# A recurrent gate's state part as seven block products: TensorE work, setup on GpSimd, and a new start order in a graph network kernel

## Chip, cores and metric

The kernel runs on one core of one Trainium2 chip. The metric is the device time of that core in microseconds (us), the median of several runs. All data are 32-bit floats.

## The reference

There are 128 graphs of 128 nodes with 256 features. Three graph attention layers come first, then a gated graph network of three steps. Each of the four layers works on a normalised copy and adds its result to `x`.

```python
h = jnp.maximum(_layernorm(x, axis=-1), 0.0)
x = x + _L0_gnn_ref(h, adj, ...)          # attention, three times with own weights
...
def _gru_cell(inp, h, w_ih, w_hh, b_ih, b_hh):
    gi = inp @ w_ih.T + b_ih
    gh = h @ w_hh.T + b_hh
    i_r, i_z, i_n = jnp.split(gi, 3, axis=-1)
    h_r, h_z, h_n = jnp.split(gh, 3, axis=-1)
    r = jax.nn.sigmoid(i_r + h_r)
    z = jax.nn.sigmoid(i_z + h_z)
    n = jnp.tanh(i_n + r * h_n)
    return (1.0 - z) * n + z * h
...
for i in range(L):                        # L = 3
    m = jnp.einsum('bnd,de->bne', h, weight[i])
    aggr = jnp.einsum('bst,bsd->btd', A, m)
    h = _gru_cell(aggr, h, w_ih, w_hh, b_ih, b_hh)
```

The term `h_n`, the state's part of the candidate gate, is what the change is about. It is a product of the state (256 features by nodes) with a 256 x 256 matrix.

## The kernel before

**Groups.** Batches are handled in 33 groups: one of two batches, 31 of four, one of two. A group of four has 4 x 128 = 512 columns, so a step of the recurrent network on it is a full step; the two small groups have 256 columns and take half steps. There are 93 full and 6 half steps. Groups are counted from 0, so the third group is g = 2.

**Attention** (`attention`, three layers a group): statistics of x (bn_stats on VectorE, `ve` and `rs` on GpSimd, `nm` on VectorE), normalised rows `xn` on ScalarE, scores `scr`, a spread of one score row over the partitions through DRAM (`de`, `er`), softmax on `em`, a transpose through DRAM (`d_at`, `at`), the products `ahp` and `hp` on TensorE, and the addition to x. The first two groups do their transposes on TensorE instead of through DRAM. After the third layer the rows are normalised once more to `hn`. For g = 0 they are turned on TensorE, for the others through DRAM (`tr_h`, `d_h`, `h<-d_h`), and `flat` (L857) copies the result to the state `h` in rows of features.

**A step** (`step` inside `gru`): `aggregate` makes `agp` and its copy `ag`; `gates` (L940) makes the two gates r and z; `hidden_n` (L980) makes `h_n` in two banks `nn`; `candidate` (L1006) adds the products of `ag` to r times h_n in the banks `ni`; then the mixing gives the new state. Between steps the state goes through DRAM (`tr_hn`, `d_hn`, `hn`).

The gates use a scheme of seven block products. Weights are cut into 2 x 2 blocks of 128 x 128, the columns of h into two halves of H = 256. Instead of eight block products there are seven, of sums and differences of blocks. The combined weights are made once in the setup (`combinations`, blocks 0 to 6 of `whh_rz` and `wc_rz`). The differences of the data (`t13`, `t24`) are made for each step. The partial sums are formed in the PSUM banks a, e and b: a copy of one bank to another (L1058), a copy to s7 (L1063), two sums on VectorE (L1066, L1072) and accumulating products. `h_n` is made directly: for each of two output halves two products of 512 columns (K = 256 in two parts).

**PSUM.** Eight banks: two "gat", three "gru" (a, e, nn), two "seed" (b, ni), one "tr". A seed bank has been marked once, so that products add to what another engine wrote into it.

**Order.** Every operation is recorded with an engine, a cost and a rank, and a planner (`Plan.issue`) lays out the instructions of each engine in advance: of the operations that could start within 0.1 us of the first, the one of lowest rank is taken. No operation is taken whose rank is more than `AHEAD` above the lowest one still open. Buffers are rings: a value takes a slot when its last user is done. Ranks come from `start(g, i) = 3 g + 2 i` for the steps and `3 g - lead(g) + 2 l` for the attention, with `LEADS` for the first groups and `LEAD` for the rest; `quick = rank - URGENT` serves the short operations between products. Each engine then runs its own list in order.

Of the kernel before, what the change touches and what calls it, by code (L numbers as in the profile page):

```python
# [39 lines left out]
class Plan:  # L40
# [6 lines left out]
    WINDOW = 0.1  # L47
    AHEAD = 6.0

# [136 lines left out]
def kernel(  # L186
# [53 lines left out]
    def const_val(name, shape):  # L240
        return plan.val(const, name, 1, lambda: const.tile([P, *shape], FT, name=name))
# [21 lines left out]
    def dve(cols):  # L263
        return 0.145 + cols / 960
# [85 lines left out]
    def blocks_of(name):  # L350

        rz = const_val(f"{name}_rz", [7, 2 * P])
        n = const_val(f"{name}_n", [KD, D])
        raw = val(su, "raw", [KD, 2 * D], f"{name}_raw")
        return rz, n, raw
# [13 lines left out]

    def combinations(blocks):  # L370

        rz, n, raw = blocks

        def low(k):
            return raw.t[:, k, :].rearrange("p (g c o) -> p g c o", g=2, c=KD)[:, :, 0, :]

        def of(i):
            return rz.t[:, i, :].rearrange("p (g o) -> p g o", g=2)

        def both(i, a, b, op, reads):  # L380
            return add("DVE", dve(D), SETUP, lambda: nc.vector.tensor_tensor(
                of(i), a(), b(), op=op), reads=reads, writes=[(rz, i)])

        return [
            both(4, lambda: low(0), lambda: low(1), OP.add, [raw]),
            both(6, lambda: of(0), lambda: low(0), OP.subtract, [(rz, 0), raw]),
            both(5, lambda: of(4), lambda: of(0), OP.subtract, [(rz, 4), (rz, 0)]),
            both(2, lambda: of(1), lambda: of(5), OP.subtract, [(rz, 1), (rz, 5)]),
            add("DVE", dve(D), SETUP, lambda: nc.vector.tensor_scalar(
                of(3), low(1), -1.0, None, op0=OP.mult), reads=[raw], writes=[(rz, 3)]),  # L390
        ]
# [32 lines left out]
    def hidden():  # L424
        blocks = blocks_of("whh")
        ld, _ = loaded(w_hh, "whh")

        def part(k):
            ps = bank("gru", f"whh_{k}")
            turned_rows(ps, ld, k, 0, 4, blocks)  # L430
            kept(ps, k, blocks, "whh")
            pn = bank("gru", f"whhn_{k}")
            turned_rows(pn, ld, k, 4, 2, blocks)
            add("ACT", act(D), SETUP, lambda: nc.scalar.mul(
                blocks[1].t[:, k, :], pn.t[:, :D], 0.25), reads=[pn], writes=[(blocks[1], k)])

        for k in range(KD):
            part(k)
        return blocks

    WHH = hidden()
    combinations(WHH)
    wih = val(su, "wih", [KD, O3], "wih", bufs=1)
    transposed(w_ih, wih, "wih")

    def combined(i):
        gt = val(su, "gt", [KD, D], f"gt_{i}")
        transposed(gweight[i], gt, f"gt{i}")
        blocks = blocks_of(f"wc_{i}")

        def product(ps, m, o0, n):
            def one(k):
                add("PE", pe(n), SETUP, lambda: nc.tensor.matmul(
                    ps.t[:, :n], gt.t[:, k, m * P : (m + 1) * P], wih.t[:, k, o0 : o0 + n],
                    start=(k == 0), stop=(k == KD - 1),
                ), reads=[gt, wih], writes=[ps], takes=blocks)

# [12 lines left out]
        return blocks, [part(m) for m in range(KD)] + combinations(blocks)  # L470

    WC, last_setup = [], []
    for i in range(STEPS):
# [104 lines left out]
    def attention(g, l, xt, cap):  # L578

        name, n = f"{g}_{l}", SIZES[g]  # L580
        rank = 3.0 * g - lead(g) + 2.0 * l
        xn = val(gw, "xn", [G, D], f"xn_{name}", bufs=XN, cut=n)
# [169 lines left out]
    def gat(g):  # L752
        b0, n = FIRST[g], SIZES[g]
        rank = 3.0 * g - lead(g)
        xt = val(grp, "x", [G, D], f"x_{g}", bufs=5, cut=n)
        adj_t = val(grp, "adj", [G, N], f"adj_{g}", dtype=I32, cut=n)
# [10 lines left out]
        for l in range(3):  # L767
            attention(g, l, xt, cap)
        rank = 3.0 * g - lead(g) + 5.5
        hn = val(gw, "xn", [G, D], f"hn_{g}_0", bufs=XN, cut=n)  # L770
# [43 lines left out]
    def gru(g, xt, am, hn0, h0):  # L814
# [48 lines left out]
        def step(i, h):  # L863
# [15 lines left out]
            s7, c22 = (val(None, v, [T], f"{v}_{name}", bufs=1) for v in ("s7", "c22"))  # L879
            nn = [bank("gru", f"nn_{name}_{c}") for c in range(KD)]  # L880
            ni = [bank("seed", f"ni_{name}_{c}") for c in range(KD)]
# [20 lines left out]
            def sums(v, tag, at):  # L902
# [29 lines left out]
                }  # L932

            def gates(ps, blk, what, at, early, starts, takes=()):

# [40 lines left out]

            def hidden_n(c):
                for k in range(KD):
                    def fn(k=k):
                        nc.tensor.matmul(  # L980
                            nn[c].t[:, :TG], WHH[1].t[:, k, c * P : (c + 1) * P], h.t[:, k, :TG],
                            start=(k == 0), stop=(k == KD - 1))
                    op = add("PE", pe(TG), rank + NNR + 0.04 * c, fn, reads=[WHH[1], (h, k)],
                        writes=[nn[c]], after=gone, takes=[*takes, wn[c]])
                    if k == 0:
                        begun.append(op)
                cn = 2 * KD + c
                add("ACT", act(TG) + 0.05, quick, lambda: nc.scalar.activation(
                    wn[c].t[:, :TG], nn[c].t[:, :TG], AF.Identity, bias=bh.t[:, cn : cn + 1]
                ), reads=[nn[c], bh], writes=[wn[c]])  # L990

# [61 lines left out]
            for k in range(KD):  # L1053
# [5 lines left out]
                reads=[a], writes=[b], after=seeds)  # L1059
            for c in range(KD):  # L1060
                hidden_n(c)
            gates(e, 6, "t3", rank + 0.15, rank + 0.12, True)
# [28 lines left out]
        def end(h):  # L1091
            rank = start(g, STEPS - 1) + 1.5
            far = g < NG - FAR
# [28 lines left out]

    URGENT = 2.0
    XN = 4
    begun, seeded = [], []
    RB, ZB, NB, HB, H0 = 2, 2, 2, 2, 2
    NNR = 0.3
    LEAD = 8.50
    LEADS = [9.00, 9.50, 8.00, 8.00, 7.75, 7.75]

    def lead(g):

        return LEADS[g] if g < len(LEADS) else LEAD

    def start(g, i):

        return 3.0 * g + 2.0 * i

# [44 lines left out]
```

## Time and profile before

| what | value |
|---|---|
| median of 3 runs | 2620.41 us (2620.08 to 2621.71) |
| profiled execution | 2615.51 us |
| its span, first to last instruction | 2613.7 us |
| TensorE busy | 2569.9 us |
| VectorE, ScalarE, GpSimd busy | 2048.0, 1732.4, 216.2 us |
| products of h_n (L980) | 792 records, 379.3 us |
| mean granted TensorE clock | 0.992 |

One product of 32-bit floats leaves two records of TensorE. Records overlap, since products are pipelined, so the distance from start to start says more than the mean duration. In the lists of instructions, "idle before" is the time in which the engine stood still just ahead of the group, with the instruction that ended it. In the windows view PEclk is the granted clock as a share of the full one.

### The profile page before, as it was taken

To read this page: it belongs to the slowest core of one execution; us is meant where nothing else is said; L and a number is where in the kernel's file an instruction comes from. 1 tells how busy PE (TensorE), PEld (TensorE's weight loads), DVE (VectorE), ACT (ScalarE), POOL (GpSimd) and SP (SyncE) were. 2 spreads that over 40 slices of the span, in tenths; PEclk is the share of its full clock that TensorE was granted. 3 is DMA by queue.
4 is the path that set the end of the run, shared out by engine and by line. 5 is a ranking of instruction groups with operands and counts; after the bars stand their busy time and mean duration, and the time that the engine had idled before them with its cause. 6 is when DMAs were issued, how large, how long until landed. Compare 5 with 4: busy or idle time off the path is not lost.

```text
span 2613.7 us, 37277 instructions
## 1 busy us (share of the span) xinstructions
PE 2569.9 (98%) x11955; PEld 1994.0 (76%) x11955; DVE 2048.0 (78%) x4777; ACT 1732.4 (66%) x4112; POOL 216.2 (8%) x303
## 2 busy tenths in 40 slices
PE   8898999999999999999999999999999999999998
PEld 5776777777777777777777777777777777777777
DVE  6776878888878888878888878888878888877654
ACT  6766666766666766666766666776666766665544
POOL 1100000000010100010100010100010100000000
PEclk8998999999999999999999999999999999999999
DMA  3122334333433433333433433433333433333320
GB/s 104 49 57 65 105 105 114 98 92 93 111 100 105 109 90 94 111 100 104 109 92 92 111 101 102 109 97 89 110 101 105 106 97 91 108 91 90 74 61 13
DMA packets 503114, 245.63 MB, mean 94 GB/s; under 512 B 280579, under 2 KB 472067, under 8 KB 502918
## 3 DMA queue, kind: packets, MB, share of 16 engines
q1 hardware_dynamic: 502918, 243.25, 35.1%
q8 instruction: 95, 1.56, 0.3%
q14 instruction: 101, 0.83, 0.1%
HBM read 139.28 MB, written 103.87 MB: 93 GB/s over the span
## 4 chain that ended last, share of the span: by engine, by line
PE 92%; ACT 1%; DMA 0%; DVE 0%; SPq 0%; issue 0%; DVEq 0%; ACTq 0%
PE b L940 19%; PE a L940 12%; PE e L940 12%; PE ni L1006 12%; PE nn L980 12%; PE hp L728 12%; PE agp L966 6%; PE ahp L709 6%; DMA at<-d_at 0%; DMA er<-de 0%; SPq L549 0%; PE hnp L838 0%; ACT em L652 0%; ACT xn L588 0%; ACT em L665 0%
## 5 line engine op out<-in xcount | busy, mean ns | idle before, releaser
L980 PE MATMUL nn<-h,whh_n 128*128 128x512 f32 (+1 forms) x792 | 379.3, 581 | 0.1
L1006 PE MATMUL ni<-ag,wc_n 128*128 128x512 f32 (+1 forms) x792 | 361.8, 580 | 1.5 <-DVE ni L1000 1.5
L728 PE MATMUL hp<-w,ah 128*128 128x256 f32 x1536 | 361.6, 382 | 0.2 <-ACT ah L716 0.2
L728 PEld LDWEIGHTS hp<-w,ah 128*128 128x128 f32 x1536 | 282.4, 190 | 43.9 <-ACT ah L716 6.9
L966 PEld LDWEIGHTS agp<-am,hn 128*128 128x128 f32 x1536 | 228.6, 192 | 98.5 <-issue 80.8
L596 DVE SCALAR_TENSOR_TENSOR scr<-xn,va 128x256 f32<-128x256 f32 x732 | 271.2, 418 | 34.9 <-ACT xn L588 34.5
L966 PE MATMUL agp<-am,hn 128*128 128x128 f32 x1536 | 237.0, 276 | 6.9 <-ACT ag L974 3.6
L940 PE MATMUL a<-h,whh_rz 128*128 128x256 f32 (+1 forms) x792 | 209.9, 376 | 9.0 <-DVE h L857 8.8
L1006 PEld LDWEIGHTS ni<-ag,wc_n 128*128 128x128 f32 x792 | 140.6, 191 | 97.3 <-issue 87.3
L511 POOL TENSOR_SCALAR ve<-st 128x4 f32<-128x4 f32 (+1 forms) x132 | 39.8, 301 | 2079.9 <-DVE st L505 1475.5
L742 ACT ACTIVATE t<-hp 128x512 f32<-128x512 f32 x192 | 104.6, 595 | 156.0 <-PE hp L728 153.0
L588 ACT ACTIVATE xn<-x,nm,rs 128x256 f32<-128x256 f32 x366 | 200.6, 591 | 4.5 <-DVE nm L517 4.0
L1011 ACT ACTIVATE wn<-ni,bi 128x512 f32<-128x512 f32 (+1 forms) x198 | 133.5, 674 | 104.1 <-PE ni L1006 100.7
L940 PE MATMUL a<-ag,wc_rz 128*128 128x256 f32 (+1 forms) x792 | 200.6, 375 | 0.0
L709 PEld LDWEIGHTS ahp<-at,xn 128*128 128x128 f32 x1536 | 184.8, 192 | 15.1 <-issue 6.2
L980 PEld LDWEIGHTS nn<-h,whh_n 128*128 128x128 f32 x792 | 149.8, 191 | 59.9 <-issue 44.0
L709 PE MATMUL ahp<-at,xn 128*128 128x128 f32 x1536 | 188.4, 275 | 4.5 <-DMA at<-d_at 2.7
L744 DVE SCALAR_TENSOR_TENSOR x<-hp,x 128x512 f32<-128x512 f32 x192 | 124.1, 686 | 86.5 <-ACT t L742 86.3
L1000 DVE SCALAR_TENSOR_TENSOR ni<-r,wn 128x512 f32<-128x512 f32 (+1 forms) x198 | 135.1, 683 | 58.1 <-ACT r L994 44.9
L635 ACT ACTIVATE em<-er,e 128x128 f32<-128x128 f32 x366 | 172.3, 521 | 5.1 <-DMA er<-de 5.1
L505 DVE BATCH_NORM_STATS2 st<-x 128x6 f32<-128x512 f32 x256 | 172.1, 689 | 2.7 <-DMA x<-in_x_dram 2.6
L652 ACT ACTIVATE em<-em,nmx 128x128 f32<-128x128 f32 x384 | 149.4, 392 | 34.1 <-DVE nmx L648 33.9
(138 smaller groups left out, 5016.0 us busy)
## 6 DMA issues: line engine op xcount, KB each, us to landing
d_hn<-tr_hn SPq DMA_DIRECT2D x116, 256.0 KB, 2.4
hn<-d_hn SPq DMA_DIRECT2D x464, 64.0 KB, 2.5
er<-de SPq DMA_DIRECT2D x90, 256.0 KB, 4.4
d_at<-tr_at SPq DMA_DIRECT2D x90, 256.0 KB, 2.0
at<-d_at SPq DMA_DIRECT2D x360, 64.0 KB, 2.0
x<-in_x_dram SPq DMA_DIRECT2D x31, 512.0 KB, 5.6
d_h<-tr_h SPq DMA_DIRECT2D x31, 512.0 KB, 2.8
h<-d_h SPq DMA_DIRECT2D x124, 128.0 KB, 2.8
```

The lines of the kernel that those rows point to most:

```text
L505: add("DVE", dve(T), rank, lambda: nc.vector.bn_stats(st.t[:, b, :].rearrange("p b s -> p (b s)"), xt.t[:, b, :].rearrange("p b d -> p d b ...
L588: add("ACT", 0.45, rank, lambda: nc.scalar.activation(xn.t[:, b, :], xt.t[:, b, :], AF.Relu, bias=nm.t[:, b : b + 1], scale=rs.t[:, b : b ...
L596: add("DVE", dve(D), rank, lambda: nc.vector.scalar_tensor_tensor(scr.t, xn.t[:, b, :], 1.0 if far else rs.t[:, b : b + 1], VA[l].t[:, s, ...
L635: add("ACT", 0.55 if far else 0.42, rank, lambda: nc.scalar.activation(em.t[:, b, :], e2_row(b), AF.Prelu, bias=e.t[:, 0, b : b + 1], alph ...
L652: add("ACT", 0.42, rank, lambda: nc.scalar.activation(em.t[:, b, :], em.t[:, b, :], AF.Exp, bias=nmx.t[:, b : b + 1], accum_out=sm.t[:, b ...
L709: add("PE", pe(P), rank, lambda: nc.tensor.matmul(summed(ps, b), xn.t[:, b, k * P : (k + 1) * P], turned_weights(b), start=True, stop=True ...
L728: add("PE", pe(D), rank, lambda: nc.tensor.matmul(hp.t[:, b * D : (b + 1) * D], ah.t[:, k, c * P : (c + 1) * P], W[l].t[:, k, :], start=(k ...
L940: nc.tensor.matmul(ps.t[:, gate * D : gate * D + H], w[0].t[:, blk, gate * P : (gate + 1) * P], rhs(), start=go, stop=w is not WHH, skip_g ...
L966: nc.tensor.matmul(ps.t[:, b * P : (b + 1) * P], s, am.t[:, b, :], start=True, stop=True)
L980: nc.tensor.matmul(nn[c].t[:, :TG], WHH[1].t[:, k, c * P : (c + 1) * P], h.t[:, k, :TG], start=(k == 0), stop=(k == KD - 1))
L1000: op = add("DVE", dve(TG), quick, lambda: nc.vector.scalar_tensor_tensor(ni[c].t[:, :TG], r[c].t[:, :TG], 1.0, wn[c].t[:, :TG], op0=OP.add ...
L1006: add("PE", pe(TG), rank + 0.45 + 0.05 * c, lambda k=k: nc.tensor.matmul(ni[c].t[:, :TG], WC[i][1].t[:, k, c * P : (c + 1) * P], ag.t[:, k ...
```

## The change

- `h_n` is made by the same scheme of seven products of 256 columns, in one "gru" bank (`ae`) and one "seed" bank (`bb`), with two copies on ScalarE, two sums on VectorE and three activations of 256 columns in place of two of 512.
- `combinations` also makes the blocks of the candidate gate from w_hh, and runs on GpSimd instead of VectorE.
- The order: `AHEAD` 6 to 3.5, `URGENT` 2 to 1, `LEADS` for the first ten groups (the third from 8.0 to 10.5), layers 2.25 apart instead of 2, new starts for the first four groups, six buffers of x instead of five, four of wn instead of two.

```diff
-    AHEAD = 6.0
+    AHEAD = 3.5
...
-        n = const_val(f"{name}_n", [KD, D])
+        n = const_val(f"{name}_n", [7, P] if name == "whh" else [KD, D])
...
-    def combinations(blocks):
+    def combinations(to, raw, gates):
...
-            return add("DVE", dve(D), SETUP, lambda: nc.vector.tensor_tensor(
-                of(i), a(), b(), op=op), reads=reads, writes=[(rz, i)])
+            return add("POOL", pool(gates * P), SETUP, lambda: nc.gpsimd.tensor_tensor(
+                of(i), a(), b(), op=op), reads=reads, writes=[(to, i)])
...
+        raw_n = val(su, "raw_n", [KD, D], "whh_raw_n", bufs=1)
...
             add("ACT", act(D), SETUP, lambda: nc.scalar.mul(
-                blocks[1].t[:, k, :], pn.t[:, :D], 0.25), reads=[pn], writes=[(blocks[1], k)])
+                raw_n.t[:, k, :], pn.t[:, :D], 0.25), reads=[pn], writes=[(raw_n, k)])
+            add("ACT", act(P), SETUP, lambda: nc.scalar.mul(
+                n.t[:, k, :], pn.t[:, P : 2 * P], 0.25), reads=[pn], writes=[(n, k)])
...
-        return blocks
-
-    WHH = hidden()
-    combinations(WHH)
+        return blocks, combinations(rz, raw, 2) + combinations(n, raw_n, 1)
+
+    WHH, last_setup = hidden()
...
-        rank = 3.0 * g - lead(g) + 2.0 * l
+        rank = 3.0 * g - lead(g) + SPAN * l
...
-        xt = val(grp, "x", [G, D], f"x_{g}", bufs=5, cut=n)
+        xt = val(grp, "x", [G, D], f"x_{g}", bufs=6, cut=n)
...
-            nn = [bank("gru", f"nn_{name}_{c}") for c in range(KD)]
+            s7n = val(None, "s7n", [D], f"s7n_{name}", bufs=1)
+            ae, bb = bank("gru", f"nn_{name}"), bank("seed", f"nnb_{name}")
...
-            def hidden_n(c):
-                for k in range(KD):
-                    def fn(k=k):
-                        nc.tensor.matmul(
-                            nn[c].t[:, :TG], WHH[1].t[:, k, c * P : (c + 1) * P], h.t[:, k, :TG],
-                            start=(k == 0), stop=(k == KD - 1))
...
+            def hidden_n():
...
+                at = rank + NNR
+                one(ae, 0, 0, "11", at, True, takes)
+                one(ae, D, 6, "t3", at, False)
+                add("ACT", act(H), quick, lambda: nc.scalar.copy(bb.t[:, :H], ae.t[:, :H]),
+                    reads=[ae], writes=[bb], after=seeds)
+                add("ACT", act(H), quick, lambda: nc.scalar.copy(s7n.t[:, :H], ae.t[:, D : D + H]),
+                    reads=[ae], writes=[s7n])
+                one(bb, 0, 5, "t2", at + 0.01, False)
+                one(ae, 0, 1, "21", at + 0.02, False)
+                keep(1, 0, ae, 0)
+                add("DVE", dve(H), quick, lambda: nc.vector.tensor_add(
+                    ae.t[:, D : D + H], bb.t[:, :H], s7n.t[:, :H]), reads=[bb, s7n], writes=[ae])
+                one(bb, 0, 4, "t1", at + 0.03, False)
+                add("DVE", dve(H), quick, lambda: nc.vector.scalar_tensor_tensor(
+                    wn[0].t[:, H : 2 * H], bb.t[:, :H], bias(0), s7n.t[:, :H], op0=OP.add, op1=OP.add,
+                ), reads=[bb, s7n, bh], writes=[(wn[0], 1)])
+                one(ae, D, 3, "t4", at + 0.04, False)
+                keep(0, 0, ae, D)
+                one(bb, 0, 2, "22", at + 0.05, False)
+                keep(1, 1, bb, 0)
...
-    URGENT = 2.0
+    URGENT = 1.0
+    BASES = [0.00, 3.00, 6.00, 9.00]
+    GAPS = [2.00, 2.00, 2.25, 2.00]
+    SPAN = 2.25
+    HEAD = 5.5
+    TAIL = 1.5
...
-    RB, ZB, NB, HB, H0 = 2, 2, 2, 2, 2
-    NNR = 0.3
-    LEAD = 8.50
-    LEADS = [9.00, 9.50, 8.00, 8.00, 7.75, 7.75]
+    RB, ZB, NB, HB, H0 = 2, 2, 4, 2, 2
+    NNR = 0.25
+    LEAD = 8.5
+    LEADS = [7.50, 9.00, 10.50, 7.00, 7.75, 7.25, 8.50, 8.50, 8.50, 8.50]
...
-        return 3.0 * g + 2.0 * i
+        return BASES[g] + GAPS[g] * i if g < len(BASES) else 3.0 * g + 2.0 * i
```

Here `one(ps, o, blk, what, ...)` is one product of block `blk` of the state's weights with the data `what` into columns from `o` of a bank, and `keep(c, s, ps, o)` moves a finished quarter of h_n with its bias into `wn` on ScalarE.

More of the change, by code (lines that the diff above doesn't have):

```diff
@@ L368, in kept @@
         ), reads=[ps], writes=[(rz, m)])
-    def combinations(blocks):
-        rz, n, raw = blocks
+    def combinations(to, raw, gates):
         def low(k):
-            return raw.t[:, k, :].rearrange("p (g c o) -> p g c o", g=2, c=KD)[:, :, 0, :]
+            return raw.t[:, k, :].rearrange("p (g c o) -> p g c o", g=gates, c=KD)[:, :, 0, :]
         def of(i):
-            return rz.t[:, i, :].rearrange("p (g o) -> p g o", g=2)
+            return to.t[:, i, :].rearrange("p (g o) -> p g o", g=gates)
         def both(i, a, b, op, reads):
-            return add("DVE", dve(D), SETUP, lambda: nc.vector.tensor_tensor(
-                of(i), a(), b(), op=op), reads=reads, writes=[(rz, i)])
+            return add("POOL", pool(gates * P), SETUP, lambda: nc.gpsimd.tensor_tensor(
+                of(i), a(), b(), op=op), reads=reads, writes=[(to, i)])
         return [
             both(4, lambda: low(0), lambda: low(1), OP.add, [raw]),
[L386 to L390, printed above, removed]
+            both(6, lambda: of(0), lambda: low(0), OP.subtract, [(to, 0), raw]),
+            both(5, lambda: of(4), lambda: of(0), OP.subtract, [(to, 4), (to, 0)]),
+            both(2, lambda: of(1), lambda: of(5), OP.subtract, [(to, 1), (to, 5)]),
+            add("POOL", pool(gates * P), SETUP, lambda: nc.gpsimd.tensor_scalar(
+                of(3), low(1), -1.0, None, op0=OP.mult), reads=[raw], writes=[(to, 3)]),
         ]
@@ L425, in hidden @@
         blocks = blocks_of("whh")
+        rz, n, raw = blocks
+        raw_n = val(su, "raw_n", [KD, D], "whh_raw_n", bufs=1)
         ld, _ = loaded(w_hh, "whh")
@@ L432, in part @@
             pn = bank("gru", f"whhn_{k}")
-            turned_rows(pn, ld, k, 4, 2, blocks)
+            turned_rows(pn, ld, k, 4, 2, [*blocks, raw_n])
             add("ACT", act(D), SETUP, lambda: nc.scalar.mul(
-                blocks[1].t[:, k, :], pn.t[:, :D], 0.25), reads=[pn], writes=[(blocks[1], k)])
+                raw_n.t[:, k, :], pn.t[:, :D], 0.25), reads=[pn], writes=[(raw_n, k)])
+            add("ACT", act(P), SETUP, lambda: nc.scalar.mul(
+                n.t[:, k, :], pn.t[:, P : 2 * P], 0.25), reads=[pn], writes=[(n, k)])
         for k in range(KD):
             part(k)
-        return blocks
-    WHH = hidden()
-    combinations(WHH)
+        return blocks, combinations(rz, raw, 2) + combinations(n, raw_n, 1)
+    WHH, last_setup = hidden()
     wih = val(su, "wih", [KD, O3], "wih", bufs=1)
@@ L468, in part @@
                 blocks[1].t[:, m, :], pn.t[:, :D], 0.5), reads=[pn], writes=[(blocks[1], m)])
-        return blocks, [part(m) for m in range(KD)] + combinations(blocks)
-    WC, last_setup = [], []
+        return blocks, [part(m) for m in range(KD)] + combinations(blocks[0], blocks[2], 2)
+    WC = []
     for i in range(STEPS):
@@ L768, in gat @@
             attention(g, l, xt, cap)
-        rank = 3.0 * g - lead(g) + 5.5
+        rank = 3.0 * g - lead(g) + HEAD
         hn = val(gw, "xn", [G, D], f"hn_{g}_0", bufs=XN, cut=n)
@@ L932, in sums, with one @@
                 }
+            def one(ps, o, blk, what, at, starts, takes=()):
+                rhs, rkey = bh_[what]
+                op = add("PE", pe(H), at, lambda: nc.tensor.matmul(
+                    ps.t[:, o : o + H], WHH[1].t[:, blk, :], rhs(),
+                    start=starts, stop=True, skip_group_check=True,
+                ), reads=[WHH[1], rkey], writes=[ps], after=gone, takes=[*takes, *wn])
+                if starts:
+                    begun.append(op)
             def gates(ps, blk, what, at, early, starts, takes=()):
@@ L975, in aggregate, with bias, keep @@
                     reads=[ps], writes=[(ag, k)])
-            def hidden_n(c):
-                for k in range(KD):
-                    def fn(k=k):
-                        nc.tensor.matmul(
-                            nn[c].t[:, :TG], WHH[1].t[:, k, c * P : (c + 1) * P], h.t[:, k, :TG],
-                            start=(k == 0), stop=(k == KD - 1))
[L983 to L990, printed above, removed]
+            def hidden_n():
+                def bias(c):
+                    return bh.t[:, 2 * KD + c : 2 * KD + c + 1]
+                def keep(c, s, ps, o):
+                    add("ACT", act(H) + 0.03, quick, lambda: nc.scalar.activation(
+                        wn[c].t[:, s * H : (s + 1) * H], ps.t[:, o : o + H], AF.Identity, bias=bias(c)
+                    ), reads=[ps, bh], writes=[(wn[c], s)])
+                at = rank + NNR
[18 more added lines that the diff above has]
+                keep(1, 1, bb, 0)
@@ L1059, in step @@
                 reads=[a], writes=[b], after=seeds)
-            for c in range(KD):
-                hidden_n(c)
+            hidden_n()
             gates(e, 6, "t3", rank + 0.15, rank + 0.12, True)
@@ L1091, in end @@
         def end(h):
-            rank = start(g, STEPS - 1) + 1.5
+            rank = start(g, STEPS - 1) + TAIL
             far = g < NG - FAR
```

## The prediction

> **What bounds the kernel now.** I read the page from the top: the busy rows and the forty slices, the chain, then the costliest groups.
>
> ```profile
> PE 2569.9 (98%) x11955; PEld 1994.0 (76%) x11955; DVE 2048.0 (78%) x4777; ACT 1732.4 (66%) x4112; POOL 216.2 (8%) x303
> PEclk8998999999999999999999999999999999999999
> PE 92%; ACT 1%; DMA 0%; DVE 0%; SPq 0%; issue 0%; DVEq 0%; ACTq 0%
> L980 PE MATMUL nn<-h,whh_n 128*128 128x512 f32 (+1 forms) x792 | 379.3, 581 | 0.1
> ```
>
> TensorE is busy 98% and carries 92% of the chain that ended last. The state's candidate products (nn, L980) wait for nothing: 0.1 us in 792 records. But busy TensorE is not TensorE at its peak, so I took the windows view next: busy time per stretch, TensorE, weight loads, VectorE, ScalarE, GpSimd, then granted clock.
>
> ```profile
> 50.00:100.00 50.00, 42.45 (x219) 34.14 (x218) 40.56 (x129) 38.04 (x111) 5.62 (x9) 0.90 0.10 27
> 200.00:300.00 100.00, 92.41 (x427) 72.66 (x426) 73.14 (x165) 62.02 (x149) 7.53 (x12) 0.93 0.36 95
> 1200.00:1500.00 300.00, 300.00 (x1383) 232.02 (x1382) 243.23 (x552) 203.84 (x476) 25.69 (x34) 1.00 0.39 103
> ```
>
> From about 300 to 2560 us TensorE never stops and has its full clock; there a product removed is time removed. In the first 300 us it stands idle and its clock drops. The chain repeats a group every 78.26 us (the row "hp L728 x16" at 1074.39, 1152.66, 1230.93). The timeline of TensorE gives the pitch of a product, which the mean ns of a pipelined record does not:
>
> ```profile
> 1014.94 1.03 PE L940 MATMUL b<-t13h,whh_rz 128*128 128x256 f32 x4
> 1015.80 1.03 PE L940 MATMUL b<-t13a,wc_rz 128*128 128x256 f32 x4
> 1016.66 1.88 PE L980 MATMUL nn<-h,whh_n 128*128 128x512 f32 x4
> 1018.38 1.03 PE L940 MATMUL e<-t24h,whh_rz 128*128 128x256 f32 x4
> ```
>
> Each f32 product leaves two records. From start to start, two products of 512 columns take 1.72 us (16.66 to 18.38), so 0.860 each; four of 256 take 1.72 (14.94 to 16.66), so 0.431 each. Eight of 128 (ahp x16) take 1.79: 0.224 each.
>
> **What the Trainium skill says.** "TensorE: Matmul & The Clock Gate", What's actually happening: after an idle window of about 3.4 us the array falls to half its clock until it has been busy for such a window. The trace agrees: after a 6.92 us gap at 210.90 four records of 256 columns take 2.08 us, elsewhere 1.03. The same page, Architectural detail: VectorE and ScalarE are strictly first in, first out, so an instruction that waits holds all behind it; this is how I read the orders below. "GPSIMD Engine Reference", 3.1: a two-input elementwise operation costs about 2.6 cycles an element against VectorE's one. No run shown here has one of this size on GpSimd.
>
> **Products.** A full step (four batches; 31 groups x 3 = 93) has four nn products of 512 columns: 3.44 us. It gets seven of 256: 3.02. Saved 0.42 (0.414 by the unrounded pitch of the chain's rows), so 38.5 to 39. The six half steps: 4 x 0.431 - 7 x 0.224 = 0.16, together 1. **Sum: -39.5 us**, 1.24 a group, so the period becomes 77.0. Nothing else must be removed for this: the differences t13, t24 of h exist already for the gates.
>
> **ScalarE and VectorE.** A step loses two activations of 512 (0.687, L988). It gains two copies of 256 (0.37, as L974 in its half form) and three activations of 256 (0.47, L988 in its half form): +0.78. VectorE gains two operations of 256 at 0.43 (as L908): +0.86. By group: ScalarE 53.2 + 2.3 = 55.5 of 77.0 (72%), VectorE 63.5 + 2.6 = 66.1 (86%). Neither becomes the bound; cover is TensorE itself. Costed at nothing as throughput, not as waits.
>
> **New waits.** Three hand-offs a step now stand between the products of one bank: copy to bb, then t2; VectorE's sum, then t4; VectorE's sum into wn, after which block 22 may write bb. In the built program's order, in steady state, the work that TensorE has between the two ends is 5 us or more, 2.6 or 2.15, and 1.29 twice and 0.86 once a group. The same kind of hand-off in the trace: VectorE starts 0.2 us after the last product streamed, takes 0.43, and TensorE goes on 0.06 later (e L1066 at 2601.31, b at 2601.80): 0.69. So even the tightest fits, by 0.17 us, unless VectorE is inside another operation (0.6 to 0.7 us) or waits for GpSimd's rs. What is behind it is all of VectorE's queue, and TensorE behind that. Lower bound 0; upper 0.3 us for each of those three hand-offs a group, 28 us in all. I take 0.1 a group, **+3**.
>
> **Banks.** The step takes three "gru" banks instead of four and four "seed" banks instead of three. The ring of two makes ni_0 take b's bank and wait for the two tanh that read it. In steady state 2.6 us of other products stand between (agp, a, e of the next step); I count 2.3 for the two tanh, the seeding ni (L1000) and hand-overs. In the last step nothing stands between: **+1.5**.
>
> **Setup.** Fifteen 256-wide VectorE operations of 0.42 and five of 0.29 (8 us) leave a VectorE that is 70 to 85% busy there, and 25 operations go to GpSimd: by the skill 2.6 x 256 / 1.2 GHz = 0.56 us plus some 0.2, so an estimate of about 15 us in 40 us, GpSimd's 10% busy being the cover. The rs of the first groups stand behind bursts of five (3 to 4 us). Two more copies on ScalarE, 0.3 each. Bounds: -3 to +4; taken as 0.
>
> **Order of the start.** The third group (g = 2) has its costliest wait in the trace before:
>
> ```profile
> PE a L940 <- DVE h L857: 8.8, 2, 6.9
> 199.63 1.60 PE L966 MATMUL agp<-am,hn 128*128 128x128 f32 x8 [2.78 <-ACT hn L956]
> 201.90 2.08 PE L966 MATMUL agp<-am,hn 128*128 128x128 f32 x8 [0.68 <-ACT ag L974]
> 210.90 2.08 PE L940 MATMUL a<-h,whh_rz 128*128 128x256 f32 x4 [6.92 <-DVE h L857]
> ```
>
> Its last attention product ended at 187.2; its state came through the DMA exchange at 210.4: 23 us, for which TensorE had 11.3 us of work. Idle and half clock cost some 13 to 15 us. In the new order 38 us of work stand there: this stall goes. But the order shows what is late next: the **fourth** group's last attention product stands 3.4 us of work ahead of its agp and 5.2 ahead of its first gate (42 us before). From the rows: x 2.6, six mixing operations 3.9 that stand ahead of bn_stats 1.3, GpSimd 1.7, four ACTIVATE 2.1, the transposes 1.3, two DMA trips 2.4 and 4.5, the copy 0.8, hand-overs: about 21 us. So some 16 us idle and 3 at half clock, about 19 lost: the stall moves by one group. Before that, the second group's early layers win perhaps 5 to 6 us of the 12 lost between 70 and 100 (the third group's first layer fills the wait for h), and the third group's second layer, about 30 us after its first with 16 us of work between, may give half back. Taken together -1, from -15 to +13. The moved layers take seven DMAs each (de, er, d_at, four at) earlier on SP's queue and two operations of stats earlier on GpSimd's. Their number is the same, and at 50 to 100 us the DMAs move 27 GB/s (windows), so they meet nothing; but GpSimd's bursts of the setup stand in the same queue, which is in the bounds above. The sixth buffer of x lets loads start sooner, at no cost I can find.
>
> **Sum** against the profiled execution (2615.5, of which the span 2613.7): -39.5 + 3 + 1.5 + 0 - 1 = -36 to -37, 2579 us. The median shown is 2620.4, 5 above that execution; from it 2583.5. I forecast **2583**.
>
> **Rivals.**
> A, the stall vanishes instead of moving: the start gives 15 us more and the hand-offs cost nothing; 2620.4 - 39.5 - 13 = **2567**. For it: TensorE idles 31 us in the first 300. Against: the cover of 5.2 us for the fourth group.
> B, half the gain is eaten: hand-offs at their upper bound or a start worse by 13, with VectorE at 86%: about **2600**. For it: the 0.86 us cover. Against: in 300 to 2400 us the old order, laid out by the same plan, lost under 5 us to all waits.
> C, slower: VectorE's in-order queue becomes the bound of every step. Place: bb's sums at L1009 and L1012 of the new program behind nm, which waits for GpSimd. It decides from 0.42 us of stall a step (40 us / 96); at 0.55 the time is about **2633**. For it: three hand-offs a step. Against: two of the three have over 1.2 us of cover almost everywhere.
> That the products are not shortened is excluded by the program's order, which has seven of 256 columns a step.
>
> **Chances.** A measurement of this kernel can tell about 0.2%, 5 us, from no change. The forecast 0.60 (its own range 2574 to 2593), A 0.14, B 0.19, C 0.05, and 0.02 for no change. Faster 0.93, same 0.02, slower 0.05. The range leaves out C and the outer parts of A and B: 2565 to 2602.
>
> **What would show it.** Right: the nn group with 1386 records of which 1302 are 256 wide, its busy share lower; the chain's period near 77.0; TensorE at 300 of 300 in the middle windows; no 6.9 us wait at the third group but one of 8 us or more for hn and for h at the fourth, with the clock near 0.5 in that 10 us window. Wrong: a period of 77.5 or more, or nn and nnb waiting for VectorE or ScalarE by tens of us; or a first 300 us in which TensorE idles under 20 us (A) or over 45 (B).

## The result, and the profile after

The changed kernel takes **2607.53 us** (median of 4 runs, 2604.89 to 2608.94) against 2620.24 us for the kernel before measured beside it (2619.53 to 2621.71): the ratio is 0.995, 95% interval 0.9932 to 0.9967. So it is 12.7 us faster, where 37 were forecast (2583, range 2565 to 2602). The profiled execution takes 2606.36 us and its span is 2604.6 us, 9.1 below the span before.

The page of the changed kernel, read in the same order as that of the kernel before: the busy row, then the chain that ended last.

```profile
PE 2535.1 (97%) x12549; PEld 2104.6 (81%) x12549; DVE 2105.3 (81%) x4955; ACT 1768.6 (68%) x4411; POOL 225.8 (9%) x328
...
PE 94%; DVE 3%; ACT 2%; DMA 0%; issue 0%; SPq 0%; POOL 0%; ACTq 0%; DVEq 0%; POOLq 0%
```

TensorE works 35 us less than before, but the span is only 9 us shorter; 26 us of the difference have become idle time. The chain gives the first hint where: VectorE had 0% of it and has 3% now. The lines by which the page ascribes that (scr L597, x L745, st L506) belong to the attention.

The windows view of the changed kernel places it. The columns are those of the windows shown in the prediction: TensorE, weight loads, VectorE, ScalarE, GpSimd, granted clock, DMA share and GB/s.

```profile
50.00:100.00 50.00, 32.53 (x141) 24.08 (x140) 27.47 (x79) 30.44 (x92) 13.10 (x18) 0.83 0.11 32
100.00:150.00 50.00, 36.41 (x227) 32.15 (x226) 29.62 (x90) 26.26 (x74) 6.44 (x9) 0.86 0.14 41
310.00:322.00 12.00, 4.35 (x16) 3.76 (x16) 5.85 (x20) 6.75 (x18) 1.05 (x1) 0.50 0.72 177
1200.00:1500.00 300.00, 300.00 (x1480) 250.45 (x1479) 254.82 (x590) 209.83 (x520) 25.48 (x36) 1.00 0.40 104
```

The middle is as forecast: TensorE 300 of 300 us at full clock, VectorE 85%, ScalarE 70%. From 50 to 100 us TensorE lost 10 us of busy time against the 42.45 before, from 100 to 150 us another 12 (48.38 before). The 1480 records in the middle window against 1383 are the new products of half the width. The chain of the changed kernel gives the period of a group, and TensorE's timeline the pitch of a new product:

```profile
1000.05 3.45 PE hp L729 x16
...
1076.89 3.45 PE hp L729 x16
```

```profile
1008.52 0.59 PE L939 MATMUL nnb<-t24h,whh_n 128*128 128x256 f32 x2
1008.95 0.59 PE L939 MATMUL nn<-h,whh_n 128*128 128x256 f32 x2
```

The period is 76.84 us (1076.89 - 1000.05), before 78.26; one product (two records) takes 0.43 us from start to start (1008.95 - 1008.52). The products of the candidate gate, asked for by tile, wait for almost nothing:

```profile
L939 PE MATMUL nnb<-t24h,whh_n x198: 273/379/483, 108.9 to 2588.1; 128*128 128x256 f32 x186, 128*128 128x128 f32 x12
...
  DVE nn L1009: 0.8, 1
  ACT nnb L1002: 0.5, 1
```

The last two lines are TensorE's idle time just before the products into `nnb`, in the whole span, with what ended it.

**Work and loss.** To compare executions with different products I count in each stretch the products of each width times their pitch (512 columns 0.8585, 256 columns 0.4315, 128 columns 0.2235 us: the pitches of the prediction with one digit more, from the rows of the chain, as 3.45 us for the eight products of hp). The rest of the stretch is loss: idle time, and inside the busy time what a lowered clock adds and what products lose that do not follow each other at this pitch. In us:

| stretch | before | after | difference |
|---|---|---|---|
| work in the whole span | 2531.8 | 2492.4 | -39.4 |
| loss 0 to 150 | 37.6 | 65.3 | +27.7 |
| loss 150 to 330 | 17.4 | 25.3 | +7.9 |
| loss 330 to 600 | 6.7 | 5.9 | -0.8 |
| loss 600 to 2400 | 6.9 | 2.7 | -4.2 |
| loss after 2400 | 10.3 | 10.3 | 0 |

The sum of the differences is -8.8, and the span fell by 9.1. The work is a count times a pitch, so its fall alone proves nothing. But from 600 to 2400 us of the changed kernel the same pitches account for 1797.3 of 1800 us, so the new products do run at the pitch that was assumed. The products gave what was worked out, and the start took some 35 us back. The waits of TensorE in the first 330 us of the changed kernel (total, times, longest, in us) say at what:

```profile
PE atp L682 <- ACT em L666: 8.5, 3, 5.5
PE agp L978 <- ACT hn L778: 7.5, 1, 7.5
PE e L625 <- DVE scr L597: 7.3, 3, 5.7
PE ahp L710 <- DMA at<-d_at: 7.2, 1, 7.2
PE a L952 <- DVE h L858: 6.7, 1, 6.7
```

Two of them (agp on hn, a on h) are the fourth group's stall, as TensorE's timeline shows; the brackets are the idle time ahead of the instruction and what ended it:

```profile
310.40 2.27 PE L978 MATMUL agp<-am,hn 128*128 128x128 f32 x8 [7.48 <-ACT hn L778]
...
322.15 2.08 PE L952 MATMUL a<-h,whh_rz 128*128 128x256 f32 x4 [6.72 <-DVE h L858]
```

The third group's stall, 6.92 us before, is gone. The other three waits belong to attention chains of the first three groups. In the kernel before the first of them was 0.2 us, the one for scr 1.7 us, and there was none for `at` coming through DRAM.

### The profile page after: what moved, and what is told of

Read it like the earlier page. It is cut to its first block, busy times and chain, and to the rows that moved or that the text cites. A ratio compares the mean times of both kernels' runs of the same rounds, so it can differ in the third digit from the quotient of the medians.

```text
span 2604.6 us, 39011 instructions
## 1 busy us (share of the span) xinstructions
PE 2535.1 (97%) x12549; PEld 2104.6 (81%) x12549; DVE 2105.3 (81%) x4955; ACT 1768.6 (68%) x4411; POOL 225.8 (9%) x328
## 4 chain that ended last, share of the span: by engine, by line
PE 94%; DVE 3%; ACT 2%; DMA 0%; issue 0%; SPq 0%; POOL 0%; ACTq 0%; DVEq 0%; POOLq 0%
PE b L952 19%; PE hp L729 13%; PE ni L1034 12%; PE a L952 12%; PE e L952 12%; PE ahp L710 7%; PE agp L978 6%; PE nn L939 6%; PE nnb L939 5%; DVE scr L597 0%; DVE x L745 0%; DVE st L506 0%; DVE x L747 0%; PE hnp L839 0%; ACT em L653 0%
## 5 line engine op out<-in xcount | busy, mean ns | idle before, releaser
L1034 PE MATMUL ni<-ag,wc_n 128*128 128x512 f32 (+1 forms) x792 | 353.1, 583 | 4.1 <-DVE ni L1028 4.1
L597 DVE SCALAR_TENSOR_TENSOR scr<-xn,va 128x256 f32<-128x256 f32 x732 | 269.8, 417 | 35.9 <-ACT xn L589 35.5
L1034 PEld LDWEIGHTS ni<-ag,wc_n 128*128 128x128 f32 x792 | 148.5, 192 | 130.8 <-issue 105.5
L978 PEld LDWEIGHTS agp<-am,hn 128*128 128x128 f32 x1536 | 206.2, 193 | 50.6 <-issue 30.4
L978 PE MATMUL agp<-am,hn 128*128 128x128 f32 x1536 | 211.8, 277 | 10.8 <-ACT hn L778 7.5
L710 PEld LDWEIGHTS ahp<-at,xn 128*128 128x128 f32 x1536 | 192.7, 197 | 27.1 <-issue 20.4
L512 POOL TENSOR_SCALAR ve<-st 128x4 f32<-128x4 f32 (+1 forms) x132 | 28.5, 216 | 2117.1 <-DVE st L506 1822.7
L745 DVE SCALAR_TENSOR_TENSOR x<-hp,x 128x512 f32<-128x512 f32 x192 | 124.1, 686 | 93.8 <-ACT t L743 93.6
L506 DVE BATCH_NORM_STATS2 st<-x 128x6 f32<-128x512 f32 x256 | 171.2, 690 | 2.6 <-DMA x<-in_x_dram 2.4
L636 ACT ACTIVATE em<-er,e 128x128 f32<-128x128 f32 x366 | 163.7, 522 | 6.1 <-DMA er<-de 6.1
L952 PEld LDWEIGHTS a<-h,whh_rz 128*128 128x128 f32 x792 | 141.0, 191 | 27.2 <-DVE h L858 10.6
L952 PEld LDWEIGHTS a<-ag,wc_rz 128*128 128x128 f32 x792 | 141.1, 191 | 15.1 <-issue 0.5
L717 ACT COPY ah<-ahp 128x512 f32<-128x512 f32 (+1 forms) x198 | 113.3, 573 | 56.8 <-PE ahp L710 50.6
```

What stands on the lines that cost most here:

```text
L506: add("DVE", dve(T), rank, lambda: nc.vector.bn_stats(st.t[:, b, :].rearrange("p b s -> p (b s)"), xt.t[:, b, :].rearrange("p b d -> p d b ...
L597: add("DVE", dve(D), rank, lambda: nc.vector.scalar_tensor_tensor(scr.t, xn.t[:, b, :], 1.0 if far else rs.t[:, b : b + 1], VA[l].t[:, s, ...
L636: add("ACT", 0.55 if far else 0.42, rank, lambda: nc.scalar.activation(em.t[:, b, :], e2_row(b), AF.Prelu, bias=e.t[:, 0, b : b + 1], alph ...
L710: add("PE", pe(P), rank, lambda: nc.tensor.matmul(summed(ps, b), xn.t[:, b, k * P : (k + 1) * P], turned_weights(b), start=True, stop=True ...
L952: nc.tensor.matmul(ps.t[:, gate * D : gate * D + H], w[0].t[:, blk, gate * P : (gate + 1) * P], rhs(), start=go, stop=w is not WHH, skip_g ...
L978: nc.tensor.matmul(ps.t[:, b * P : (b + 1) * P], s, am.t[:, b, :], start=True, stop=True)
```

## The experiments

Two theories stood against each other (O and S in the first expectations below). **Order**: the seven products give 39 us wherever TensorE has no gap, and the start's new order spends most of it. **Products**: what is lost comes with the products themselves (their hand-offs, more work for VectorE, the setup on GpSimd) and no order would keep it. Losses below are counted as in the table above.

### The new products with the order of before

```diff
-    AHEAD = 3.5
+    AHEAD = 6.0
-    URGENT = 1.0
+    URGENT = 2.0
-    SPAN = 2.25
+    SPAN = 2.0
-    NNR = 0.25
+    NNR = 0.3
-    LEADS = [7.50, 9.00, 10.50, 7.00, 7.75, 7.25, 8.50, 8.50, 8.50, 8.50]
+    LEADS = [9.00, 9.50, 8.00, 8.00, 7.75, 7.75]
-        return BASES[g] + GAPS[g] * i if g < len(BASES) else 3.0 * g + 2.0 * i
+        return 3.0 * g + 2.0 * i
```

Five buffers of x instead of six, too.

> The changed kernel with its seven products and GpSimd setup, but every number of the order put back (AHEAD 6, URGENT 2, SPAN 2, starts 3g + 2i, old LEADS, NNR 0.3, five buffers of x). Theory O (the new order of the start costs what the products gain): the products bring 39 us and nothing takes it back, 2580 to 2586 us, first 330 us as before (TensorE idle there about 31 us). Rival S (the new setup and the new products themselves slow the start): still 2600 to 2608.

Measured: 2764.32 us, ratio 1.055 (1.0534 to 1.0566): 144 us **slower** than before, where one theory expected 2580 to 2586 and the other 2600 to 2608: both missed. The first 150 us lose 46.1, well under the changed kernel's 65.3, but every 600 us of the middle lose 45 to 49. TensorE's window from 600 to 1200 us and its longest wait from 600 to 2400 us:

```profile
600.00:1200.00 600.00, 570.81 (x2736) 466.34 (x2735) 471.41 (x1088) 392.32 (x957) 51.03 (x66) 0.98 0.36 96
```

```profile
PE a L952 <- DVE h L858: 40.2, 10, 8.3
```

The waits are not at the new hand-offs (nn, nnb) but at the old places: the state `h` of the next group (40.2 us in 10 waits) and the transposed `at` (20.9 us in 8) come late in every second or third group. The edit takes a buffer of x away too. That does not look like the cause: the first statistics of a group (L506), which wait for its load, start mostly 23 to 35 us after it here, against 17 us in the kernel before. So with these products the order of before no longer covers its own attention; the numbers of the order are part of what makes the products pay, not an addition to them.

### The old products with the new order

The kernel before, with all the numbers of the new order and six buffers of x, as the edit above read backwards.

> The kernel before with only the order's numbers of the change (AHEAD, URGENT, SPAN, starts, LEADS, NNR, six buffers of x). Theory O: slower by 25 to 36 us, 2645 to 2656. Rival S: 2617 to 2624, no change.

Measured: 2672.68 us, ratio 1.0199 (1.0184 to 1.0214): slower, as the order theory said, but by 52 us, more than its 25 to 36. Its start, with no new product in it and no combination on GpSimd, waits at the same places, for nearly the same times, as the changed kernel's (waits of TensorE, first 330 us):

```profile
PE atp L681 <- ACT em L665: 8.7, 3, 6.0
PE ahp L709 <- DMA at<-d_at: 8.2, 1, 8.2
PE e L624 <- DVE scr L596: 7.4, 3, 5.7
PE a L940 <- DVE h L857: 6.8, 1, 6.8
```

Its loss in the first 330 us is 89.7, the changed kernel's 91.0. **The new order alone, without a new product, costs the start as much.** With the order of before the new products do cost the start something: the run above loses 70.7 in 330 us, the kernel before 55.4. The two do not add up in the changed kernel. In the middle this kernel loses 10 to 13 us per 600: the new order suits the old products badly too, if less so than the old order suits the new ones. The whole times do not add up either: alone the two parts cost 144 and 52 us, together they gain 13.

### The combinations on VectorE again

```diff
-            return add("POOL", pool(gates * P), SETUP, lambda: nc.gpsimd.tensor_tensor(
+            return add("DVE", dve(gates * P), SETUP, lambda: nc.vector.tensor_tensor(
...
-            add("POOL", pool(gates * P), SETUP, lambda: nc.gpsimd.tensor_scalar(
+            add("DVE", dve(gates * P), SETUP, lambda: nc.vector.tensor_scalar(
```

> The changed kernel with the weights' combinations back on VectorE (25 operations), all else as changed. Theory O: GpSimd's bursts are off the path of the start, 2602 to 2612. Rival S in its GpSimd form (rs of the first groups waits behind the bursts): 2585 to 2595.

Measured: 2610.35 us (2608.91 to 2611.53), in the range of the order theory (2602 to 2612). The ratio is 0.9962 (0.9947 to 0.9977), against 0.995 (0.9932 to 0.9967) for the changed kernel. The intervals overlap, so the 2.8 us between the medians are not told from nothing; the start loses 93.1 in 330 us instead of 91.0. The move to GpSimd is not where the gain went.

### The old leads alone

```diff
-    LEADS = [7.50, 9.00, 10.50, 7.00, 7.75, 7.25, 8.50, 8.50, 8.50, 8.50]
+    LEADS = [9.00, 9.50, 8.00, 8.00, 7.75, 7.75]
```

> The changed kernel with the LEADS of before (9.0, 9.5, 8.0, 8.0, 7.75, 7.75), all else of the new order kept. Theory O1 (the leads of the first four groups carry the loss: third group early, fourth late): 2583 to 2592. O2 (AHEAD, URGENT or SPAN carry it): 2600 to 2612.

Measured: 2621.18 us, ratio 1.0001 (0.9993 to 1.001): no faster than before, so both expectations missed. The start gets much better (first 150 us: 48.6 instead of 65.3; 150 to 330: 21.4 instead of 25.3), then 330 to 600 loses 20.2 instead of 5.9 and the middle 24 instead of 2.7. The leads of the first groups reach through the whole run: the ranks from the seventh group (g = 6) on are the same in both kernels, and still TensorE is busy for 596.51 us from 600 to 1200 where it had 600.00. Of the 24 us lost in the middle 10.5 are idle time, nearly all of it before products that wait for VectorE's and ScalarE's short operations inside the gates (b for ScalarE's copy L1086, 6.5 us in 12 waits); the rest lies inside the busy time.

### The third group's lead back to 8, and the fourth group's raised to 8

Two kernels, each the changed one with one number altered:

```diff
-    LEADS = [7.50, 9.00, 10.50, 7.00, ...
+    LEADS = [7.50, 9.00, 8.00, 7.00, ...      third
+    LEADS = [7.50, 9.00, 10.50, 8.00, ...     fourth
```

> The changed kernel with the lead of the third group alone put back from 10.5 to 8.0. Theory P (the first leads fix the pattern that every later group repeats, and are paid for in the start): the first 150 us lose 10 to 20 less, but the middle windows lose 5 to 10 in each 300 us; 2615 to 2665. Rival Q (the leads matter in the start alone): 2585 to 2600.

> The changed kernel with the lead of the fourth group alone from 7.0 to 8.0. Both theories: the stall of TensorE on the fourth group's state near 300 to 322 us (17 us) goes. Theory P: the middle windows lose 3 to 10 in each 300 us in exchange, 2605 to 2660. Rival Q: 2588 to 2596.

Measured: third 2630.38 us, ratio 1.0037 (1.0024 to 1.005); fourth 2624.2 us, ratio 1.0018 (1.0011 to 1.0025). Both slower than the changed kernel, and yet each takes away just the loss it aims at. Windows of the changed kernel, then of the third's lead at 8, then of the fourth's lead at 8 (which has 595.74 of 600 us in the last window of the third's):

```profile
0.00:150.00 150.00, 111.00 (x546) 86.12 (x547) 90.22 (x280) 88.51 (x254) 35.32 (x57) 0.85 0.22 65
150.00:330.00 180.00, 161.33 (x821) 134.56 (x820) 136.32 (x340) 123.36 (x316) 14.63 (x20) 0.95 0.31 82
```

```profile
0.00:150.00 150.00, 123.81 (x611) 97.22 (x612) 97.61 (x295) 98.47 (x283) 33.87 (x55) 0.91 0.25 71
...
600.00:1200.00 600.00, 595.95 (x2904) 490.81 (x2903) 498.38 (x1166) 418.01 (x1024) 50.05 (x68) 1.00 0.39 103
```

```profile
150.00:330.00 180.00, 175.28 (x917) 147.44 (x916) 139.56 (x345) 123.15 (x307) 14.94 (x20) 1.00 0.29 81
```

With the third group's attention later, the first group reaches its first gate at 86.30 us instead of 98.41 (74.62 before the change), and the first 150 us lose 51.8 instead of 65.3: **13.5 us of the early loss come from the third group's attention being pulled ahead** of the first two. With the fourth group's attention earlier, its stall vanishes and the loss from 150 to 330 us falls from 25.3 to 7.8: **the fourth group's stall costs 17.5 us.** But both give it back later: 330 to 600 us loses 14.3 and 15.4 instead of 5.9, and 600 to 2400 us 27.0 and 25.8 instead of 2.7. What seems to decide is whether the start ends in an arrangement that repeats without a gap.

### Five buffers of x

```diff
-        xt = val(grp, "x", [G, D], f"x_{g}", bufs=6, cut=n)
+        xt = val(grp, "x", [G, D], f"x_{g}", bufs=5, cut=n)
```

> The changed kernel with five buffers of x instead of six. Theory P (the new order keeps six groups' x alive, and the steady state depends on it): TensorE waits in every group, 2660 us or more, the middle windows below 295 of 300. Rival Q (the sixth buffer does nothing, as the prediction said): 2603 to 2612.

Measured: 2884.79 us, ratio 1.1011 (1.0993 to 1.103): 277 us slower than the changed kernel, by one buffer. The start is the same (loss in 330 us 90.5); from 1200 us on a group takes 90 us. SyncE's timeline shows the store of a finished group and the load that takes its buffer, VectorE's timeline the first statistics, which wait for that load.

```profile
1245.26 0.39 SPq L1145 DMA_DIRECT2D out_dram<-x  x1
1248.66 0.43 SPq L760 DMA_DIRECT2D x<-in_x_dram  x1
```

```profile
1257.49 0.70 DVE L506 BATCH_NORM_STATS2 st<-x 128x6 f32<-128x512 f32 x1
```

By the load at 1248.66, 18 loads and 13 stores have been issued: five groups have a buffer. In the changed kernel it is 20 loads and 14 stores (by 1254.01), so six. These counts alone do not make the ring the bound. A load follows a store within 3 to 6 us in each of these kernels, and the kernel before fills six buffers as well when it has them (next run). What tells them apart is how long the loaded data lie before they are used. With five buffers the first statistics of the group start 9 us after its load was issued, about as soon as the data can be there (a load of x lands after 5.1 us on the changed kernel's page). In the kernel before they start 17 us after it, and in the changed kernel with its six buffers 84 to 88 us, a whole period later. (There the groups begun are counted: statistics started less layers finished.)

So with five buffers a group starts when the fifth before it has been stored, and five periods make one round: 5 x 90 = 450 us, of which 437 lie between first statistics and store. In the changed kernel that part takes some 370 us, as in the kernel before (369): the new order does not use x for longer. But its five slots at a period of 76.84 would give 384 us, and the use, the 3.5 us from store to load and the landing fill that to within 3 to 7 us, an estimate from these numbers; in the kernel before 12 us were left. The first theory had the slowdown right, but not its reason: it is not that six groups need their x at once. Why a group that starts late settles at 437 us, and not nearer to 370, no run shows.

### Six buffers of x in the kernel before

The opposite edit (5 to 6) in the kernel before.

> The kernel before with six buffers of x in place of five, nothing else. Theory (a buffer is worth what the order asks of it; with the old order each group's x is made late enough to find one of five free): within 3 us of the kernel before, 2617 to 2624 us, no wait for x in either. Rival (five are tight in the old order too, and part of what the changed kernel gains comes from the sixth): faster by 5 us or more.

Measured: 2618.85 us (2617.56 to 2620.57), ratio 0.9997 (0.9989 to 1.0006). Now six groups have a buffer, and nothing is gained: the loads only come a period earlier. The sixth buffer is worth nothing to the old order and 277 us to the new one.

### URGENT back to 2

```diff
-    URGENT = 1.0
+    URGENT = 2.0
```

> The changed kernel with URGENT alone put back from 1 to 2. Theory P: the pattern of the steady state is lost, 2650 to 2720, with TensorE waiting in the middle windows. Rival Q: 2603 to 2612.

Measured, one run: 2721.16 us, just above the range of the first theory (2650 to 2720). The first 330 us lose 97, about as in the changed kernel (91); the middle loses 21 to 29 us per 600. From 600 to 2400 us TensorE stands idle for 43.5 us, 36.3 of them in 7 waits for the next group's state (`a` for `h` L858). Another of the order's numbers that can't be put back by itself.

### A start mended, the rest as in the changed kernel

The edit touches only the first groups: how far the orders may run ahead while an operation of rank under 3 is open, the spacing of layers and the place of `hn` in the first three groups, and three leads.

```diff
-            limit = by_rank[low].rank + self.AHEAD
+            limit = by_rank[low].rank + (self.AHEAD if by_rank[low].rank >= 3.0 else 8.0)
...
-        rank = 3.0 * g - lead(g) + SPAN * l
+        rank = 3.0 * g - lead(g) + (SPAN if g >= 3 else 2.0) * l
...
-        rank = 3.0 * g - lead(g) + HEAD
+        rank = 3.0 * g - lead(g) + (HEAD if g >= 3 else 6.25)
...
-    LEADS = [7.50, 9.00, 10.50, 7.00, 7.75, 7.25, 8.50, 8.50, 8.50, 8.50]
+    LEADS = [7.25, 7.50, 10.50, 9.00, 7.75, 7.25, 8.50, 8.50, 8.50, 8.50]
```

> The changed kernel with its order altered for the first groups alone: in the limit on how far the orders may run ahead, 8 in place of 3.5 while the lowest rank left is under 3; for the first three groups SPAN 2.0 in place of 2.25 and HEAD 6.25 in place of 5.5; leads of the first, second and fourth group 7.25, 7.5 and 9 in place of 7.5, 9 and 7; the third keeps its 10.5. From the fourth group on the order is asked for with the same numbers as in the changed kernel. Theory (the products deliver in the middle, the start's order spends it, and the two are separate): the start's loss of TensorE's time over the first 330 us, 91 us now, falls by some 20 (the fourth group's stall of 17 goes, as it did in the run with its lead at 8, and a part of the first two groups' delay), the middle stays at 300 of 300 us in each window: 2578 to 2594 us. Rival 1 (the wait-free middle hangs on how the start ends, so that any other start leaves waits in every group, as in the runs with one lead put back): middle windows at 296 to 299, loss of some 4 to 10 a 600 us, 2600 to 2630 us. Rival 2 (the start is bounded by the attention chains of the first groups whatever their order): start's loss stays near 90, 2603 to 2612 us.

Measured: **2592.54 us** (2591.66 to 2594.61), ratio 0.9895 (0.9879 to 0.9912): 27 us below the kernel before and 15 below the changed kernel, the fastest of all. Windows:

```profile
0.00:150.00 150.00, 119.26 (x593) 94.55 (x593) 101.88 (x308) 99.16 (x283) 35.63 (x57) 0.90 0.24 70
150.00:330.00 180.00, 170.70 (x867) 142.85 (x868) 139.59 (x345) 123.80 (x314) 16.34 (x22) 0.98 0.28 77
...
600.00:1200.00 600.00, 600.00 (x2956) 500.58 (x2955) 511.82 (x1195) 420.68 (x1038) 48.67 (x69) 1.00 0.38 103
```

The first 330 us lose 70.2, 20.8 less than the changed kernel; 330 to 600 us give 8 back (13.8 instead of 5.9), and the middle stays without a gap (2.5 us lost from 600 to 2400). The start's loss and the gapless middle can be had apart, as the theory expected (2578 to 2594). It still loses 15 us more in 330 us than the kernel before (55.4).

The losses side by side, in us, with each kernel's median:

| kernel | 0 to 150 | 150 to 330 | 330 to 600 | 600 to 2400 | time |
|---|---|---|---|---|---|
| before | 37.6 | 17.4 | 6.7 | 6.9 | 2620 |
| changed | 65.3 | 25.3 | 5.9 | 2.7 | 2607.5 |
| new products, old order | 46.1 | 24.3 | 20.8 | 139 | 2764 |
| old products, new order | 66.2 | 23.2 | 2.5 | 32.9 | 2673 |
| combinations on VectorE | 67.3 | 25.6 | 7.2 | 3.1 | 2610 |
| old leads | 48.6 | 21.4 | 20.2 | 24.1 | 2621 |
| third's lead 8 | 51.8 | 29.2 | 14.3 | 27.0 | 2630 |
| fourth's lead 8 | 68.6 | 7.8 | 15.4 | 25.8 | 2624 |
| five buffers of x | 64.1 | 26.0 | 24.2 | 219 | 2885 |
| URGENT 2 | 65.4 | 31.5 | 31.4 | 74.1 | 2721 |
| before, six buffers of x | 37.6 | 19.1 | 7.1 | 7.5 | 2619 |
| start mended | 57.6 | 12.6 | 13.8 | 2.5 | 2592.5 |

## Why the prediction was wrong

The direction was right; the size was a third of what was forecast, and the measured time lies 5.5 us above the range. Step by step:

- **Products, -39.5: right.** The work counted fell by 39.4 us, and the pitch of a product of 256 columns is still 0.43 us; the gapless middle confirms both.
- **ScalarE and VectorE, nothing: right.** VectorE has 254.82 of 300 us in the middle (85%; 86% were forecast), ScalarE 209.83 (70%; 72%).
- **New waits, +3: too high.** From 600 to 2400 us TensorE waits 0.4 us in all that the trace ascribes. The middle came out 4.2 us better than before, since the small losses of the old order are gone too, which is why the period is 76.84 and not 77.0. Rival C, VectorE's queue as the bound, is ruled out by the same number.
- **Banks, +1.5: not seen.** The loss after 2400 us is 10.3 in both.
- **Setup, 0: not contradicted.** In the new order the place of the combinations makes no difference clear of the runs' spread (2.8 us). GpSimd took 19.2 us for them where about 15 were estimated. (The operations that left VectorE are sixteen of 0.42 us and four of 0.29, not fifteen and five; the sum stays 8 us.) What the setup costs in the old order was not taken apart.
- **Order of the start, -1 (-15 to +13): this is the step that failed.** It measured about +35 (27.7 up to 150 us and 7.9 from there to 330). Of its three parts, "this stall goes" was right. The fourth group's stall was right in place and nearly in size: "about 19 lost" against 17.5, with waits of 7.48 and 6.72 us where 8 or more were named, and the clock at 0.50 between. That the clock falls to half after such an idle time is what the Trainium skill states ("TensorE: Matmul & The Clock Gate", What's actually happening), and the trace agrees once more. The third part, "the second group's early layers win perhaps 5 to 6 us of the 12 lost between 70 and 100", had the wrong sign: the first 150 us lose 27.7 us more.

The reason for the wrong sign is that I asked what the moved layers would fill on TensorE, and not what they would hold up. The setup's last products end at 56.9 us. From there to the first gate TensorE has only attention chains and the turning of the first state to work on, and these chains alternate between TensorE, VectorE (scr, st, x) and ScalarE (em, xn). No engine is full: from 56 to 98 us TensorE is busy for 24.8 us, VectorE for 22.8 and ScalarE for 26.7 (before 34.6, 32.8 and 31.8). What counts is who stands ahead in each engine's list. The third group's first layer, with its lead of 10.5, stands ahead of the end of the first group's attention:

```profile
76.84 1.99 PE L729 MATMUL hp<-w,ah 128*128 128x256 f32 x8 [0.97 <-ACT ah L717]
...
81.36 0.71 DVE L539 STREAM_TRANSPOSE tr_at<-em 128x512 f32<-128x512 f32 x1 [1.22 <-ACT em L666]
81.99 0.65 DVE L745 SCALAR_TENSOR_TENSOR x<-hp,x 128x512 f32<-128x512 f32 x1
```

The first group's last product hp (two batches, so 8 records) ends at 78.83, and its addition to x starts at 81.99, behind the softmax and the transpose `tr_at` of the third group. With the third's lead at 8 the same step takes 0.7 us instead of 3.2. Then TensorE itself runs the third group's ahp and hp from 88.82 to 96.5 us, while the first group's state h, ready at 90.40, waits for its gate. The first gate of the kernel before, then of the changed one:

```profile
74.62 1.22 PE L940 MATMUL a<-h,whh_rz 128*128 128x128 f32 x4 [1.90 <-DVE h L857]
```

```profile
98.41 0.61 PE L952 MATMUL a<-h,whh_rz 128*128 128x128 f32 x4
```

The run with the third's lead at 8 shows 13.5 us of the 27.7 to come from that one number, the run with all old leads 16.7. Two or three us more come with the other numbers of the order (48.6 with the old leads, 46.1 with the whole order of before). The last 8.5 us (46.1 against 37.6) separate the new products from the old ones in the order of before. In the new order there is no such difference (65.3 against 66.2), so these 8.5 us are not simply the products' price, and they were not taken apart further.

"The sixth buffer of x lets loads start sooner, at no cost I can find" was wrong in kind: the buffer is not an addition but a condition. Without it the changed kernel would run at 2885 us. I had asked whether transfers collide, and not how little room five buffers leave in a loop of a shorter period.

The rivals: A's sum takes 13 us where its words give the start 15, and comes to 2568; it did not happen either way. B ("a start worse by 13", 2600) had the right mechanism and too small a price for it; its sign in the profile, over 45 us of TensorE's idle time in the first 300, came out at 42.8 (300 less the busy time of the windows), with the clock at 0.85 over the first 150 us instead of 0.92 adding the rest. The range went wrong with it: it took the start's bounds from one stall in the trace of before, where the trace could not show what an order would do that it did not have.

**What stays open.** Why one lead of one early group changes how the groups repeat a thousand microseconds later is shown as a fact (third's lead, fourth's lead, old leads: 24 to 27 us in the middle against 2.7) and not explained. The planner takes what is ready first; the likely cause is that a different start leaves it a different arrangement of groups, which it then repeats. No run takes the arrangement itself apart.

## What to carry to other kernels

In the stretch where TensorE never stopped, the removed products were worth their number times their pitch. An order changed along with them has a price of its own, which has to be read in the stretch where the engine does stop, from the chain of the first group and from every engine's list that the moved work enters ahead of it. An order made by a planner is one piece: here its numbers and buffer counts fitted one set of operations and not the other, so neither half of the change could be judged by running it alone. When the middle is without a gap and the start is not, give the first groups numbers of their own: here that gave another 15 us on top of the change's 13.

## What the hardware showed that I had not expected

The combinations have four operations with two inputs to one that multiplies a single input by a constant. On VectorE, in the kernel before, the one with a single input is the cheaper: 0.29 us against 0.42. On GpSimd it is the dearer. The prediction's estimate for two inputs of 128 x 256, from the Trainium skill ("GPSIMD Engine Reference", 3.1) with some dispatch added, was 0.76 us, and it had no separate price for one input. Groups of GpSimd in the changed kernel (busy us, mean ns, then idle time before):

```profile
L379 POOL TENSOR_TENSOR wc_rz<-wc_rz 128x256 f32<-128x256 f32 x6 | 4.7, 786 | 0.2
L387 POOL TENSOR_SCALAR wc_rz<-wc_raw 128x256 f32<-128x256 f32 x3 | 3.3, 1114 | 0.0
L785 POOL TENSOR_SCALAR x<-x 128x1024 f32<-128x1024 f32 x31 | 32.6, 1053 | 133.1 <-ACT hn L778 133.1
```

Two inputs take 0.79 us, about as estimated; the multiplication takes 1.11 us. That is no rule for one input: the last line, also with one, has four times the columns in 1.05 us. What makes the multiplication slow is not shown. It was not on the path that set the end.
